# Transposing keys and tokens on TensorE instead of by DMA, and grouping the output and state products, in a gated linear attention plus mixture-of-experts kernel

## The chip, the cores and the metric

One core of a Trainium2 chip. The metric is the device time of one execution in microseconds (us); the time of a kernel is the median of several runs. The engines of the core run side by side, each through its own instructions in order: TensorE (PE, with weight loads as PEld), VectorE (DVE), ScalarE (ACT), GpSimd (POOL) and SyncE (SP), which only issues DMAs here.

## What is computed

For 4 sequences of 2048 tokens of width 256, float32 (8192 tokens): a layer norm, then a gated linear attention and a mixture of 64 experts on the same normalised tokens, and both are added to `x`.

```python
xn = layernorm(x)
q, k, v = xn @ Wq, (xn @ Wk) * DK ** -0.5, xn @ Wv        # 8 heads, DK 128, DV 64
alpha = sigmoid((xn @ Wg + bg) / 16)                      # a decay per head and token
def step(state, inp):                                     # scan over the tokens of a sequence
    state = at[..., None, None] * state + kt[..., None] * vt[:, :, None, :]
    out_t = einsum('bhk,bhkv->bhv', qt, state)
attn = (out * sigmoid(xn @ Wog)) @ Wo
# experts: top 4 of 8 groups, top 8 of 64 experts, at most 256 tokens an expert
y = (silu(xe @ w_gate[e]) * (xe @ w_up[e])) @ w_down[e]   # added back with its weight
return x + attn + moe
```

## The kernel before

The scan over tokens is done in chunks of 128 tokens. A block `s` (32 of them, `block(s)`) is 256 tokens, so two chunks `ck`; the 8 heads go in two halves of 4. One (block, half, chunk) is a unit. For every unit:

- `unit_a`: a matmul `lp` makes the logarithms of the decays between the tokens of the chunk, ScalarE's Relu and Exp make the mask factor `dc` of them (VectorE or GpSimd clears its upper triangle), and 12 matmuls make `sp`, keys times queries.
- `unit_m`: VectorE multiplies `sp` into `dc`.
- `unit_d`: the output products `od<-dc,v` and `od<-qt,state` (float32, 64 columns of the array each) and the state products `od<-vwh,kt` and `od<-vwl,kt` (f16, 128 columns), which need the keys with tokens and features exchanged, `kt`. All go into one PSUM bank `od`. VectorE takes the output out of it with the gate (`oT`), and adds the state part to the decayed state.

Around them, for the next half or block: `queries` and `keys` (each projection `pj` is 12 matmuls; ScalarE takes the high half `qh` or `k`, VectorE the low half `ql` or `k` and, for queries, `qt`, which is scaled by a table `el` that a DMA spreads over the partitions), `values`, `gate` (the `wog` projection), `split_o` (splits `oT` in two for the last product) and `output` (the product with `Wo`). Values are kept as a high and a low part, so `product` issues three matmuls: high by high, high by low, low by high.

`keys` ends with one DMA transpose on SP's queue for both chunks of a half:

```python
kt = ktp.tile([P, NCK * 2 * 4, P], F16, name="kt")
made["kt"] = nc.sync.dma_start(out=kt, in_=k.rearrange("p c a h t -> p (c a h t)"), transpose=True).ins
```

`front(b)` does the layer norm of a batch of 512 tokens (16 batches) and transposes the tokens in the same way, from `x16` into `xT`, on SP's queue; `xT` goes to DRAM and comes back block by block as `xs`. `lg` are the routing logits on `xT`.

`block` writes the order of these parts down by hand. Between them stand 12 calls of `step()` per block. In the first part of the run each `step` drives the side work of the batches: `front`, `decays` and `back` (routing), every one with its due step in the list `side`. When `side` is empty, at the start of a block, the experts begin: PSUM is shared out anew (`share_banks`: four buffers `pj` and two `mo` before, three and three after), and each step advances the experts by a stage: fetch by an indirect DMA on POOL's queue, `expert_in` (which turns the fetched tokens, `xet`, on TensorE), `expert_mid` (`gu`), `expert_out` (`yp`), `expert_add` (a scattering, adding DMA). `finish` adds a block's attention to the output. A scheduler of the framework then sets the final order on each engine out of this order and its own estimate of times; `tc.issue_after(x)` keeps what is issued in it behind the instruction `x`.

PSUM has eight banks: `sp` and `od` have one each, and six are shared between `pj` and `mo`.

Of the kernel before, what the change touches and what calls it, by code (L numbers as in the profile page):

```python
# [8 lines left out]
F32 = mybir.dt.float32  # L9
# [10 lines left out]
P = 128  # L20
NT = 8192
NTL = NT // 128
D = 256
# [48 lines left out]
def gla_moe_kernel(ctx: ExitStack, tc: tile.TileContext, x, Wq, Wk, Wv, Wo, Wg, bg, Wog,  # L72
# [250 lines left out]

    def front(b):
# [54 lines left out]
        n = 2 if b == 0 else RT  # L379
        for t in range(0, RT, n):  # L380
            made["xT"] = nc.sync.dma_start(
                out=xT[:, t:t + n].rearrange("p t a c i -> p (t a c) i"),
                in_=flat[:, t:t + n].rearrange("p t k -> p (t k)"), transpose=True).ins
        nc.sync.dma_start(out=xw_d[rows, 0:D].rearrange("(t p) d -> p t d", p=P),
                          in_=flat.bitcast(F32))
        yield True
        stored = nc.sync.dma_start(out=xT_d[b], in_=xT)
# [5 lines left out]
        for _ in range(6 if b > 2 else 1):  # L393
            yield True
# [220 lines left out]
    def expert_weights(e, m):  # L615
        w = moe["w4"].tile([P, 6, I], F32, name="w", bufs=3)
        nc.sync.dma_start(out=w[:, 0:2], in_=w_gate[e].rearrange("(c p) i -> p c i", p=P))
        nc.sync.dma_start(out=w[:, 2:4], in_=w_up[e].rearrange("(c p) i -> p c i", p=P))
        nc.sync.dma_start(out=w[:, 4:6].rearrange("p c i -> p (c i)"), in_=w_down[e])
        m["w"] = w  # L620
# [234 lines left out]
    def keys(s, half, i):  # L855
# [7 lines left out]
        if i == 1:  # L863
            kt = ktp.tile([P, NCK * 2 * 4, P], F16, name="kt")
            made["kt"] = nc.sync.dma_start(out=kt, in_=k.rearrange("p c a h t -> p (c a h t)"), transpose=True).ins
            B["kt"][half] = kt

    def unit_a(s, half, ck):

        B = blk[s]  # L870
        qh, ql, _ = B["q"][half]
        k = B["k"][half]
# [11 lines left out]
        else:  # L884
            nc.gpsimd.affine_select(out=dc, in_=dc, pattern=[[0, 4], [1, P]], compare_op=ALU.is_ge,  # L885
                                    fill=0.0, base=0, channel_multiplier=-1)
        if (s, half, ck) == (NS - 1, 1, 1):
# [5 lines left out]
        B["dc", half, ck], B["sp"] = dc, sp  # L893
# [8 lines left out]
    def unit_d(s, half, ck):  # L902

        B = blk[s]
        ch = s * NCK + ck
        first = ch % (SEQ // P) == 0
        last = (ch + 1) % (SEQ // P) == 0
        h0 = half * 4
        v, dc, qt = B["v"][ck], B["dc", half, ck], B["q"][half][2]
        od = ps_at.tile([P, 2, 2 * P], F32, name="od", bufs=1)  # L910
        op = od[:, 0].rearrange("p (j i) -> p j i", j=2)
        dp = od[:, 1].rearrange("p (h v) -> p h v", h=4)
        for j in range(2):
            for i in range(2):
                nc.tensor.matmul(op[i * DV:(i + 1) * DV, j, :], lhsT=v[:, h0 + 2 * j + i, :],  # L915
                                 rhs=dc[:, 2 * j + i, :], start=True, stop=first)
            if not first:
                for i in range(2):
                    nc.tensor.matmul(op[i * DV:(i + 1) * DV, j, :], lhsT=state[half][:, 2 * j + i, :],  # L919
                                     rhs=qt[:, ck, 2 * j + i, :], start=False, stop=True)  # L920
        if not last:
            kt, vw = B["kt"][half][:, ck * 8:ck * 8 + 8], B["vw"][ck]
            for i in range(4):
                product(dp[:, i, :], (kt[:, i, :], kt[:, 4 + i, :]),
                        tuple(t[:, h0 + i, :] for t in vw))
        if half == 0:
            B["oT"][ck] = vp_.tile([P, 4, P], F32, name="oT")
        nc.vector.scalar_tensor_tensor(  # L928
            B["oT"][ck][:, half * 2:half * 2 + 2, :], in0=B["og"][:, ck, half * 2:half * 2 + 2, :],
            scalar=1.0, in1=op, op0=ALU.add, op1=ALU.mult)  # L930
        if last:
            return
        new = w2.tile([P, 4, DV], F32, tag=f"state{half}", name=f"state{half}")
        if first:
            nc.vector.tensor_copy(new, dp)
        else:
            B["aux"].tensor_tensor(new, state[half], bc(B["wall"][half][:, ck, :], 2, DV), ALU.mult)
            nc.vector.tensor_tensor(new, new, dp, ALU.add)
        state[half] = new
# [20 lines left out]
    def finish(s):  # L960
# [14 lines left out]
        else:  # L975
            mo = xsp.tile([P, NCK, D], F32, tag="xs", name="mo")
            dst = of[rows, :].rearrange("(t p) d -> p t d", p=P)
            with tc.issue_after(made["kt"]):
# [5 lines left out]

    def block(s):


        n = s + 1 < NS
        if n:
            load_block(s + 1)  # L990
            load_el(s + 1, 0)
        unit_a(s, 0, 0)
        if n:
            queries(s, 1, 0)
        else:
            keys(s, 1, 0)
        unit_m(s, 0, 0)
        step()
        if n:
            keys(s, 1, 0)  # L1000
        else:
            keys(s, 1, 1)
        step()
        unit_d(s, 0, 0)
        if s:
            output(s - 1, 0)
# [4 lines left out]

        unit_a(s, 0, 1)
        queries(s, 1, 1 if n else 0)
        unit_m(s, 0, 1)
        step()
        if n:
            keys(s, 1, 1)
        else:
            queries(s, 1, 1)
        if n:  # L1020
            load_el(s + 1, 1)
            gate(s + 1, 0)
        step()
        unit_d(s, 0, 1)
        step()

        if not n:
            unit_a(s, 1, 0)
            unit_m(s, 1, 0)
# [182 lines left out]
```

## Time and profile before

| | |
|---|---|
| median of 3 runs | 1223.55 us (1221.69 to 1233.08) |
| profiled execution | 1225.81 us, its span 1224.0 us |
| granted TensorE clock, mean | 0.983 |
| TensorE busy | 1148.5 us (94%) |
| VectorE busy | 945.9 us (77%) |
| ScalarE busy | 745.2 us (61%) |
| GpSimd busy | 710.5 us (58%) |
| DMA | 207.15 MB, 315003 packets, 198817 of them under 512 B |

A busy TensorE is a union of pipelined matmuls, so that the time that one costs is the step from its start to the next one's, not its length. An idle time is put down to the event that ended it. In a line of a group stand source line, engine, operation, output and inputs, shape and count, then busy time in us, mean length of one in ns, and the idle time of the engine just before the group with what ended it.

### The profile page before, as it was taken

The numbers are of one execution on the slowest core, as the hardware profiler recorded it, in microseconds if no ns is written. First come the engines' busy times: TensorE is split into PE (matmuls) and PEld (weight loads), VectorE is DVE, ScalarE is ACT, GpSimd is POOL, SyncE is SP. The second block draws the span as 40 slices with busy tenths as digits, with TensorE's granted clock in tenths as the row PEclk, the third lists the DMA queues.
The fourth block names the chain that finished last, engine by engine and source line by source line (L and its number), as shares of the span: only waits on it lengthen the run. The fifth ranks groups of instructions, "written<-read, shape, count | busy, mean of one in ns | idle before, by whom it ended". The sixth has DMA issues, their size and how long they took to land.

```text
span 1224.0 us, 32353 instructions
## 1 busy us (share of the span) xinstructions
PE 1148.5 (94%) x12492; PEld 972.6 (79%) x12503; DVE 945.9 (77%) x2632; ACT 745.2 (61%) x1394; POOL 710.5 (58%) x888
## 2 busy tenths in 40 slices
PE   6889899999899999999979999999999899999998
PEld 6678677777677777787768888888888788888787
DVE  6977676787578666867868898888889778878775
ACT  5567666665566666545445666666676556655664
POOL 1376777765676677553316565466674646565642
PEclk9999999999999999999989999999999899999899
DMA  8579787777677877646667888888898988888855
GB/s 266 143 173 237 184 181 181 181 171 177 146 166 150 182 174 163 154 101 149 148 98 164 177 188 186 196 191 186 177 204 170 184 162 179 171 167 164 204 77 95
DMA packets 315003, 207.15 MB, mean 169 GB/s; under 512 B 198817, under 2 KB 285729, under 8 KB 314145
## 3 DMA queue, kind: packets, MB, share of 16 engines
q1 hardware_dynamic: 281328, 155.52, 53.6%
q0 software_dynamic: 29712, 45.89, 22.2%
q10 hardware_dynamic: 3808, 3.67, 0.9%
q8 instruction: 98, 1.61, 0.6%
q14 instruction: 57, 0.46, 0.1%
HBM read 115.98 MB, written 58.38 MB: 142 GB/s over the span
## 4 chain that ended last, share of the span: by engine, by line
PE 54%; DMA 14%; DVE 12%; POOL 7%; issue 6%; ACT 6%; SPq 1%; POOLq 0%; DVEq 0%; ACTq 0%
PE pj L269 9%; PE pj L271 9%; PE pj L270 9%; DMA kt<-k 8%; DMA el<-el_d 4%; PE od L915 3%; PE od L919 2%; PE gu L269 2%; PE gu L270 2%; PE gu L271 2%; PE xet L630 2%; DVE qt L846 2%; PE sp L269 1%; DVE k L221 1%; PE yp L269 1%
## 5 line engine op out<-in xcount | busy, mean ns | idle before, releaser
L688 POOL DMA_INDIRECT out_dram<-y,idx x128 | 210.4, 1644 | 136.4 <-DMA out_dram<-y,idx 66.6
L610 POOL DMA_INDIRECT xe<-xw_d,idx x128 | 137.0, 1070 | 120.8 <-ACT y L674 41.3
L221 DVE SCALAR_TENSOR_TENSOR ql<-pj,qh 128x512 f16<-128x512 f32 x128 | 87.1, 681 | 64.7 <-ACT qh L220 64.7
L269 PE MATMUL pj<-xs,wq_h 128*128 128x256 f16 x496 | 135.9, 274 | 0.8 <-DVE k L221 0.8
L269 PE MATMUL pj<-xs,wk_h 128*128 128x256 f16 x496 | 136.3, 275 | 0.1
L271 PE MATMUL pj<-xs,wk_l 128*128 128x256 f16 x496 | 136.1, 274 | 0.0
L270 PE MATMUL pj<-xs,wk_h 128*128 128x256 f16 x496 | 136.1, 274 | 0.0
L270 PE MATMUL pj<-xs,wq_h 128*128 128x256 f16 x496 | 135.7, 273 | 0.0
L271 PE MATMUL pj<-xs,wq_l 128*128 128x256 f16 x496 | 135.7, 273 | 0.0
L898 DVE TENSOR_TENSOR dc<-sp,dc 128x512 f32<-128x512 f32 x128 | 87.5, 684 | 43.7 <-POOL dc L885 34.0
L915 PE MATMUL od<-dc,v 128*64 128x128 f32 x1024 | 108.1, 287 | 4.2 <-DVE dc L898 3.1
L220 ACT ACTIVATE qh<-pj 128x512 f16<-128x512 f32 x128 | 76.4, 597 | 45.3 <-PE pj L271 44.8
L220 ACT ACTIVATE k<-pj 128x512 f16<-128x512 f32 x128 | 76.3, 596 | 42.3 <-PE pj L271 41.8
L269 PE MATMUL sp<-qh,k 128*128 128x128 f16 x512 | 97.4, 223 | 3.3 <-ACT k L220 2.4
L919 PE MATMUL od<-qt,state 128*64 128x128 f32 x960 | 99.3, 276 | 0.0
L270 PE MATMUL sp<-ql,k 128*128 128x128 f16 x512 | 96.9, 223 | 1.7 <-DVE ql L221 1.7
L271 PE MATMUL sp<-qh,k 128*128 128x128 f16 x512 | 97.0, 223 | 0.5 <-DVE k L221 0.4
L221 DVE SCALAR_TENSOR_TENSOR k<-pj,k 128x512 f16<-128x512 f32 x128 | 86.8, 678 | 7.9 <-ACT k L220 7.8
L928 DVE SCALAR_TENSOR_TENSOR oT<-og,od 128x256 f32<-128x256 f32 x128 | 52.9, 414 | 47.8 <-PE od L271 46.9
L879 ACT ACTIVATE dc<-lp 128x512 f32<-128x512 f32 x128 | 76.4, 597 | 21.3 <-PE lp L875 19.1
L674 ACT ACTIVATE y<-yp,xe 128x256 f32<-128x256 f32 x128 | 53.7, 471 | 58.4 <-PE yp L271 55.5
L846 DVE SCALAR_TENSOR_TENSOR qt<-pj,el 128x512 f32<-128x512 f32 x128 | 86.7, 678 | 0.0
(401 smaller groups left out, 4244.4 us busy)
## 6 DMA issues: line engine op xcount, KB each, us to landing
el<-el_d SPq DMA_DIRECT2D x64, 512.0 KB
xw_d<-x SPq DMA_DIRECT2D x16, 512.0 KB
xT_d<-xT SPq DMA_DIRECT2D x16, 512.0 KB
out_dram<-in_L_attn_x_dram SPq DMA_DIRECT2D x16, 512.0 KB
w<-in_L_ffn_w_gate_dram SPq DMA_DIRECT2D x64, 128.0 KB
w<-in_L_ffn_w_up_dram SPq DMA_DIRECT2D x64, 128.0 KB
w<-in_L_ffn_w_down_dram SPq DMA_DIRECT2D x64, 128.0 KB
xs<-xT_d SPq DMA_DIRECT2D x31, 256.0 KB
```

What stands on the lines that cost most here:

```text
L220: return (nc.scalar.activation(hi, t, AF.Copy, scale=scale).ins, nc.vector.scalar_tensor_tensor(lo, in0=t, scalar=scale, in1=hi, op0=ALU.m ...
L221: nc.vector.scalar_tensor_tensor(lo, in0=t, scalar=scale, in1=hi, op0=ALU.mult, op1=ALU.subtract).ins)
L269: nc.tensor.matmul(out_, lhsT=a[0], rhs=b[0], start=first, stop=False)
L270: nc.tensor.matmul(out_, lhsT=a[0], rhs=b[1], start=False, stop=False)
L271: return nc.tensor.matmul(out_, lhsT=a[1], rhs=b[0], start=False, stop=last).ins
L610: in_turn(lambda: nc.gpsimd.indirect_dma_start(out=xe[:, f, :], out_offset=None, in_=xw_d[:, :], in_offset=bass.IndirectOffsetOnAxis(ap=id ...
L688: two = [in_turn(lambda: nc.gpsimd.indirect_dma_start(out=of, out_offset=bass.IndirectOffsetOnAxis(ap=idx[:, e, f:f + 1], axis=0), in_=m[" ...
L846: read = nc.vector.scalar_tensor_tensor(qt, in0=pj, scalar=QFIT, in1=two_heads(el, i), op0=ALU.mult, op1=ALU.mult)
L879: nc.scalar.activation(dc, lp, AF.Relu, scale=-1.0)
L898: anchor.append(nc.vector.tensor_tensor(dc, B["sp"], dc, ALU.mult).ins)
L915: nc.tensor.matmul(op[i * DV:(i + 1) * DV, j, :], lhsT=v[:, h0 + 2 * j + i, :], rhs=dc[:, 2 * j + i, :], start=True, stop=first)
L919: nc.tensor.matmul(op[i * DV:(i + 1) * DV, j, :], lhsT=state[half][:, 2 * j + i, :], rhs=qt[:, ck, 2 * j + i, :], start=False, stop=True)
```

## The change

1. Keys: `keys` no longer issues a DMA. A new part `turn_keys(s, half, ck)` transposes the 8 key tiles of a unit on TensorE into a `pj` buffer `kp`; ScalarE copies it to `kt` (before the experts begin, ScalarE and VectorE copy a half each).
2. Tokens: `turn_tokens` transposes the 16 tiles of a batch on TensorE into two `mo` buffers `tp`, and VectorE copies each to `xT`.
3. `unit_d` is split. `outputs(units)` does the output products of two units as one run, held together by `issue_after`, in an `od` bank of their own; `states(units)` does the state products of the two afterwards, in a `pj` buffer `dp`.
4. `unit_l`, the mask factor, is taken out of `unit_a` and stands a step ahead.
5. `block` has a new order: keys first in a half block, then queries, the turned keys, values and gate; `split_o` and `output` move. The first unit stands ahead of the loop over blocks, with a `step()` of its own.

```diff
+    def turn_tokens(x16, xT):
+        for t in range(0, RT, 2):
+            tp = ps["mo"].tile([P, 2, 2, 2, P], F16, tag="mo", name="tp")
...
+                        nc.tensor.transpose(tp[:, t2, a, c, :], x16[:, t + t2, a, c * P:(c + 1) * P], identh)
+            nc.vector.tensor_copy(xT[:, t:t + 2], tp)
...
-        n = 2 if b == 0 else RT
-        for t in range(0, RT, n):
-            made["xT"] = nc.sync.dma_start(
-                out=xT[:, t:t + n].rearrange("p t a c i -> p (t a c) i"),
-                in_=flat[:, t:t + n].rearrange("p t k -> p (t k)"), transpose=True).ins
...
+        if b < 2:
+            turn_tokens(x16, xT)
...
+        if b >= 2:
+            turn_tokens(x16, xT)
+            yield True
...
-        if i == 1:
-            kt = ktp.tile([P, NCK * 2 * 4, P], F16, name="kt")
-            made["kt"] = nc.sync.dma_start(out=kt, in_=k.rearrange("p c a h t -> p (c a h t)"), transpose=True).ins
-            B["kt"][half] = kt
...
+    def turn_keys(s, half, ck):
...
+        kp = ps["pj"].tile([P, 2 * 4, P], F16, tag="pj", name="kp")
+        for i in range(2 * 4):
+            nc.tensor.transpose(kp[:, i, :], k[:, i, :], identh)
...
+        if "at" in moe:
+            nc.scalar.copy(kt, kp)
+        else:
+            nc.scalar.copy(kt[:, 0:4], kp[:, 0:4])
+            nc.vector.tensor_copy(kt[:, 4:8], kp[:, 4:8])
...
+    def outputs(units):
+
+        od = ps_at.tile([P, 2, 2, P], F32, name="od", bufs=1)
+
+        begun = ExitStack()
+        for n, (s, half, ck) in reversed(list(enumerate(units))):
...
+                    mm = nc.tensor.matmul(od[i * DV:(i + 1) * DV, n, j, :], lhsT=v[:, h0 + 2 * j + i, :],
+                                          rhs=dc[:, 2 * j + i, :], start=True, stop=first)
+                    if i == j == 0:
+                        begun.enter_context(tc.issue_after(mm.ins))
...
+    def states(units):
...
+        dp = ps["pj"].tile([P, 2, 4, DV], F32, tag="pj", name="dp")
+        for n, (s, half, ck) in enumerate(units):
+            kt, vw = blk[s]["kt"][half][:, ck * 8:ck * 8 + 8], blk[s]["vw"][ck]
+            with tc.issue_after(made["od"]):
+                for i in range(4):
+                    product(dp[:, n, i, :], (kt[:, i, :], kt[:, 4 + i, :]),
+                            tuple(t[:, half * 4 + i, :] for t in vw))
```

The new order of the first half block, in `block`:

```diff
+        states(done)
+        if s:
+            split_o(s - 1, 1)
...
+        unit_l(s, 0, 1)
+        keys(s, 1, 0)
+        step()
+        unit_a(s, 0, 1)
+        keys(s, 1, 1)
+        unit_l(s, 1, 0)
+        step()
+        unit_m(s, 0, 1)
+        queries(s, 1, 0)
+        step()
+        queries(s, 1, 1)
+        turn_keys(s, 1, 0)
+        if s:
+            output(s - 1, 1)
+        step()
...
+        if n:
+            values(s + 1, 0)
+        unit_a(s, 1, 0)
+        turn_keys(s, 1, 1)
+        if s:
+            gate(s, 1)
+        step()
+        unit_m(s, 1, 0)
+        done[:] = (s, 0, 1), (s, 1, 0)
+        outputs(done)
+        step()
```

The second half block has the same order for the other half of the heads, with the next block's projections.

## The prediction

> **What bounds the kernel now.** I read the page first: engine totals, then the chain of work that ended last, then the windows of 30 us, the groups by line, the waits, and last TensorE's timeline at the edges of the `od` products.
>
> ```profile
> PE 1148.5 (94%) x12492; PEld 972.6 (79%) x12503; DVE 945.9 (77%) x2632; ACT 745.2 (61%) x1394; POOL 710.5 (58%) x888
> ...
> PE 54%; DMA 14%; DVE 12%; POOL 7%; issue 6%; ACT 6%; SPq 1%; POOLq 0%; DVEq 0%; ACTq 0%
> ```
>
> TensorE is busy for 1148.5 of 1224.0 us and holds most of the chain. Only 75.5 us of it are idle, so added TensorE work is paid in full unless it takes the place of a wait. The windows (columns: span, busy time and instructions of PE, PEld, DVE, ACT, POOL, granted clock, DMA share, GB/s) show two halves:
>
> ```profile
> 450.00:480.00 30.00, 29.13 (x341) 23.57 (x339) 20.61 (x69) 19.93 (x35) 22.44 (x39) 1.00 0.68 163
> ...
> 600.00:630.00 30.00, 22.57 (x252) 19.19 (x252) 19.13 (x60) 10.51 (x19) 10.21 (x10) 0.89 0.71 114
> ...
> 660.00:690.00 30.00, 30.00 (x346) 26.48 (x343) 27.39 (x71) 18.45 (x37) 19.17 (x14) 1.00 0.87 183
> ...
> 960.00:990.00 30.00, 27.86 (x275) 24.83 (x273) 21.62 (x56) 15.10 (x32) 17.92 (x14) 0.91 0.79 151
> ```
>
> In the second half, with the experts, TensorE is full (30.00 of 30) except in a few holes, after which the granted clock falls as well (0.89, 0.91). In the first half it loses a little in every window. The groups name the waits (busy, mean ns, idle before, releaser):
>
> ```profile
> L269 PE MATMUL od<-vwh,kt 128*128 128x64 f16 x480 | 58.6, 197 | 23.1 <-DMA kt<-k 23.0
> L269 PE MATMUL pj<-xs,wog_h 128*128 128x256 f16 x248 | 67.9, 274 | 8.5 <-DVE qt L846 7.3 <-ACT res L958 1.2
> L271 PE MATMUL pj<-wo_h,ol 128*128 128x256 f32 x256 | 73.9, 289 | 6.7 <-POOL ol L946 6.5
> L269 PE MATMUL lg<-gwz,xT 128*128 128x72 f16 x128 | 14.1, 198 | 3.4 <-DMA xT<-x 3.4
> ```
>
> The holes are the state products waiting for the transposed keys: 23.0 us. The chain in order of time shows how late such a transfer lands, beside an `el` broadcast, which also fills 512 KB:
>
> ```profile
> 186.60 5.99 DMA el<-el_d
> ...
> 607.79 15.61 DMA kt<-k
> ```
>
> **What the change adds on TensorE.** 32 blocks x 2 halves x 2 chunks x 8 key tiles are 1024 transposes, and 16 batches x 16 token tiles are 256: 1280, each with its own weight load; the built order has exactly these more. The experts' inputs are turned in the same way (f16, 128x128):
>
> ```profile
> 1006.31 0.28 PE L271 MATMUL yp<-wh,hl 128*128 128x256 f32 x1
> 1006.43 0.62 PE L630 MATMUL xet<-identh,xe 128*128 128x128 f16 x8
> 1006.98 0.44 PE L919 MATMUL od<-qt,state 128*64 128x128 f32 x4
> 1007.25 0.39 PE L915 MATMUL od<-dc,v 128*64 128x128 f32 x4
> 1007.47 0.39 PE L919 MATMUL od<-qt,state 128*64 128x128 f32 x4
> 1007.79 0.20 PE L269 MATMUL od<-vwh,kt 128*128 128x64 f16 x1
> ```
>
> One takes 220 ns, but they are pipelined: 8 take 0.62 us, so the step is (0.62 - 0.22) / 7 = 0.057; I use 0.056, the step of `sp`, which has the same shape (three in 0.17 in the same timeline). 1280 x 0.056 = +71.7 us. TensorE executes in order, so all of it lies on the path where TensorE is full.
>
> The Trainium skill, "TensorE: Matmul & The Clock Gate", Part 4, puts such a transpose at about 275 ns in a kernel and says that it does not count as work for the clock gate. Taken as a spacing, 1280 x 0.275 would be 352 us; the row above gives 0.056, and the window from 660 to 690, which holds `xet` runs, has a granted clock of 1.00, so the row decides.
>
> **Output products as one group.** `od<-dc,v` and `od<-qt,state` use 64 columns (128*64), all around them 128. Inside, a group of four records steps by 0.22 (1007.25 to 1007.47); at the exit it is 0.32 (1007.47 to 1007.79), +0.10; at the entry 0.21 between a projection (1005.27, step 0.11) and the first `od` (1005.48), +0.10. A visit costs 0.20 us. In the built order of before there are 148 visits, mostly of 8 instructions and some broken up; in that of after 67, 54 of them of 16. 81 x 0.20 = -16 us. Bounds: nothing, where a visit is entered after a wait anyway, and -16.
>
> **Waits that go.** Keys: -23.0, since `kt` now comes out of a ScalarE copy that stands, in the order, ahead of the `od` group that precedes its use (bounds: -23.0, and 0 if another wait takes its place, which is R3). Tokens: -3.4. Clock: the windows after the key holes grant 0.89, 0.97, 0.91, 0.94, 0.99, 0.90; 30 x (0.11 + 0.03 + 0.09 + 0.06 + 0.01 + 0.10) = 12.0 us of clock, of which I take -9, as part of it fell on an idle TensorE (bounds -12 and 0). `output` of both chunks now stands about 9 us of TensorE work behind its `split_o`, where before the second one stood beside it: -6.5. The `wog` projection waits for a PSUM buffer that `qt` frees, and `qt` waits for `el`; on SP's queue that load now has no key transpose ahead of it (64 x 3.67 us of issue, median of the group by tile): -5 of 7.3 (bounds 0 and -7.3).
>
> The Trainium skill, "Advanced Engine Details and Errata", X-Bar Transpose (TRN2), speaks against the change: transposing DMAs are as fast as regular ones. The chain has 15.6 us for a key transfer where the equal-sized `el` took 6.0. By the rule the keys would land early enough without TensorE, the waits would have another cause, and the sum would be 1224 + 72 - 16 = 1280; I go by the rows.
>
> **Copies out of PSUM.** They are new work on the two engines beside:
>
> ```profile
> L638 DVE CAST xel<-xet 128x512 fp32r<-128x512 f16 x64 | 43.7, 683 | 1.0 <-ACT xeh L637 0.8
> L637 ACT CAST xeh<-xet 128x512 fp32r<-128x512 f16 x64 | 38.0, 593 | 10.2 <-PE xet L630 8.3 <-PE od L271 1.0 <-issue 0.3
> L377 ACT CAST x<-xt 128x1024 f16<-128x1024 f32 x14 | 14.5, 1033 | 0.0
> ```
>
> By the built order: ScalarE 66 x 0.59 + 62 x 1.03 = 103 us (745 to 848, under 70%). VectorE 66 x 0.68 = 45 and 32 token copies of 128x1024, not in the trace: between 0.68 (one of half the size) and 1.37 (two); I take 1.25, 40 us. All 85 us fall in the first half, where VectorE was busy 437 of the first 600 us (73%); it goes to about 87%. Cover: in the window 660 to 690 VectorE was at 27.39 of 30 and TensorE lost nothing, so 0 is the lower end. Queued behind such a copy are the low halves `ql`, `k` and `qt`, which free the projection's PSUM buffers, and the `dc` product that the next `od` group waits for. The upper end: TensorE's idle of the first 600 us, 49.5, less 7 for keys and tokens and 10 for the first window, is 32; a doubling costs +32. I take +5, nearer the row at 91%.
>
> PSUM: `kp` (4) and `dp` (2) join 18 other tiles per block in the `pj` pool, with 4 buffers, then 3. Waits for these buffers were only the 8.5 us of `wog`, so I price this at 0, with R3 as its other end. On SP the 81 transposes go, nothing is added; POOL's queue keeps its order, though the experts begin one block earlier (66 half copies of keys: 2 + 16 x 4).
>
> **Sum**, against the profiled execution's span: 1224.0 + 71.7 - 16 - 23.0 - 3.4 - 9 - 6.5 - 5 + 5 = 1237.8. That execution took 1225.81, 1.8 more than its span; the median, 1223.55, lies 2.3 below it. So 1237.8 + 1.8 - 2.3 = 1237 us, 1.1% slower. About 1% is also what a measurement of this kernel can tell from no change.
>
> **Rivals.**
> R1, VectorE becomes the pace of the first half. For: 87% there, in lockstep with a full TensorE through 4 PSUM buffers; the first half already waits on `ql`, `k`, `qt`. Against: 91% in the second half at no loss. Price +32 in place of +5: 1264.
> R2, not slower: the longer distances of the new order (mask factors and keys a step ahead, one `od` visit per half block) empty the remaining waits too. TensorE's idle less what I took off is 75.5 - 23 - 3.4 - 6.5 - 5 = 37.6, of which 10 are the start; if 26 go and VectorE adds nothing, 1237 - 26 - 5 = 1206. It decides from about 14 us of them on. For: those waits (`dc`, `ql`, `k`) are all first-half distances of a few matmuls. Against: VectorE's load grows there.
> R3, a wait takes the key wait's place: `kp` holds a `pj` buffer through a 1.03 us copy behind other ScalarE work. At half a copy per turn in the second half 62 x 0.5 = +31 at worst; at a third of that, 1247. Against: ScalarE is at 63% there.
>
> **How the numbers follow.** Forecast 0.40 (its own range 1224 to 1251), R1 0.22, R2 0.24, R3 0.14. Of the forecast 0.01 is faster by over 1%, 0.17 within 1%, 0.22 slower; R1 is all slower; R2 0.19 and 0.05; R3 0.07 within and 0.07 slower. Together 0.20, 0.29, 0.51. The range runs from 1208, R2 nearly whole, to 1264, R1 whole.
>
> **What would show it.** Right: `kp` and `tp` step by 0.056; the `kt` wait is gone from TensorE and the windows after 600 have clock 1.00; DMA share falls; VectorE 85 us more. The second half gets shorter and the first longer. Wrong: over 15 us of TensorE idle behind VectorE in the first half (R1), idle in all under 35 us (R2), or `pj` groups waiting on the ScalarE copy of `kt` (R3).

## The result and the profile after

The changed kernel takes 1285.84 us (median of 4 runs, 1277.83 to 1288.44); the kernel before, run beside it, 1227.99 us. The ratio is 1.0463, with a 95% interval of 1.0386 to 1.0540: slower. The forecast was 1237 us, with a range to 1264. The direction was right; the size was missed by 49 us. Of the kernels below only order_later had timed executions in a slower state with a lower granted clock (two of eight); its ratio leaves them out, its median does not.

The page of the profile after (engine busy time, one DMA queue with packets, MB and share, and the engines of the chain that ended last):

```profile
PE 1203.5 (94%) x13783; PEld 1043.5 (81%) x13783; DVE 997.4 (78%) x2733; ACT 832.4 (65%) x1522; POOL 712.1 (55%) x885
...
q1 hardware_dynamic: 114896, 113.57, 28.5%
...
PE 53%; DVE 18%; POOL 13%; ACT 6%; issue 4%; DMA 4%; SPq 1%; another core or an unknown queue 0%; POOLq 0%; DVEq 0%; ACTq 0%
```

DMA has gone from 14% of the chain to 4%, and this queue from 53.6% of the DMA engines' time to 28.5%. The line of that queue before:

```profile
q1 hardware_dynamic: 281328, 155.52, 53.6%
```

VectorE and GpSimd together now hold 31% of the chain (19% before). TensorE's idle time is 1286.7 - 1203.5 = 83.2 us, against 75.5 before, although the waits for transposed keys are gone. The same windows as before; the work in them is not quite the same, since block 16, for one, begins 48 us later in the change (span, PE, PEld, DVE, ACT, POOL, granted clock, DMA share, GB/s):

```profile
450.00:480.00 30.00, 27.71 (x340) 23.39 (x338) 23.07 (x73) 18.29 (x34) 18.98 (x31) 1.00 0.45 132
600.00:630.00 30.00, 25.50 (x250) 20.31 (x248) 26.45 (x80) 15.80 (x27) 13.96 (x15) 0.94 0.54 157
660.00:690.00 30.00, 28.66 (x309) 25.22 (x308) 23.87 (x60) 20.74 (x40) 14.25 (x11) 1.00 0.56 122
960.00:990.00 30.00, 29.63 (x335) 26.05 (x333) 24.16 (x60) 22.11 (x43) 17.06 (x13) 1.00 0.65 152
```

The hole in the last window is filled (27.86 at a clock of 0.91 before), that at 600 only in part (22.57 at 0.89 before), and windows that were full lose a little (450: 29.13, 660: 30.00 before). The groups show both sides (busy, mean ns, idle before, releaser):

```profile
L940 PE MATMUL od<-dc,v 128*64 128x128 f32 x1024 | 102.2, 282 | 9.6 <-DVE dc L924 9.6
L270 PE MATMUL sp<-ql,k 128*128 128x128 f16 x512 | 96.2, 219 | 16.5 <-DVE ql L221 15.6 <-issue 0.4
L879 PE MATMUL kp<-identh,k 128*128 128x128 f16 x1024 | 84.0, 219 | 11.2 <-DVE k L221 8.7 <-ACT dc L898 2.0 <-issue 0.4
L271 PE MATMUL pj<-wo_h,ol 128*128 128x256 f32 x256 | 72.8, 284 | 0.4 <-DVE ol L985 0.4
L269 PE MATMUL pj<-xs,wog_h 128*128 128x256 f16 x248 | 67.6, 273 | 0.4 <-ACT res L997 0.4
L269 PE MATMUL dp<-vwh,kt 128*128 128x64 f16 x480 | 50.7, 195 | 0.0
L269 PE MATMUL lg<-gwz,xT 128*128 128x72 f16 x128 | 14.7, 199 | 0.0
```

The last four lines are the waits that the forecast took off, and all four are gone. The first three are waits that were small before (below), and the `kp` group is new.

```profile
L915 PE MATMUL od<-dc,v 128*64 128x128 f32 x1024 | 108.1, 287 | 4.2 <-DVE dc L898 3.1 <-DVE state L938 0.9
L270 PE MATMUL sp<-ql,k 128*128 128x128 f16 x512 | 96.9, 223 | 1.7 <-DVE ql L221 1.7
```

**A balance of TensorE's time.** To see where the time went I followed every step from one matmul's start to the next one's. The usual step of a shape is work (0.056 us for 128x128 f16, 0.109 for 128x256 f16, 0.110 for an output product); up to 0.104 more at the edge of the 64-column products is the change of tile; what is left under a granted clock below 0.9 is half clock, except steps longer by 0.3 us or more; the rest is a stall from 0.15 us on, and small below that. I cut the run at VectorE's first `dc<-sp` product of block 0 and of block 16. What I call the first half is blocks 0 to 15, with layer norm and routing beside them; the second runs from there to the end, with the experts. All in us:

| kernel, half | length | work | of it `kp`, `tp` | tile | clock | stalls | small |
|---|---|---|---|---|---|---|---|
| before, first | 515.7 | 451.5 | 0 | 13.3 | 5.0 | 36.4 | 8.7 |
| after, first | 563.3 | 496.3 | 41.1 | 7.7 | 1.6 | 49.4 | 8.3 |
| before, second | 660.9 | 580.2 | 0 | 15.2 | 10.3 | 33.2 | 18.2 |
| after, second | 675.9 | 608.7 | 27.3 | 6.0 | 2.7 | 36.9 | 16.8 |

Both halves got longer: +47.6 and +15.0. In both, the transposes stand as work to nearly their full price, tile changes and clock give back what was forecast, and the stalls are not shorter but longer.

### The profile page after: what moved, and what is told of

The parts are those of the page before. It is cut to its first block, busy times and chain, and to the rows that moved or that the text cites. A ratio compares the mean times of both kernels' runs of the same rounds, so it can differ in the third digit from the quotient of the medians.

```text
span 1286.7 us, 34811 instructions
## 1 busy us (share of the span) xinstructions
PE 1203.5 (94%) x13783; PEld 1043.5 (81%) x13783; DVE 997.4 (78%) x2733; ACT 832.4 (65%) x1522; POOL 712.1 (55%) x885
## 3 DMA queue, kind: packets, MB, share of 16 engines
q1 hardware_dynamic: 114896, 113.57, 28.5%
## 4 chain that ended last, share of the span: by engine, by line
PE 53%; DVE 18%; POOL 13%; ACT 6%; issue 4%; DMA 4%; SPq 1%; another core or an unknown queue 0%; POOLq 0%; DVEq 0%; ACTq 0%
PE pj L269 8%; PE pj L271 8%; PE pj L270 8%; PE od L940 3%; DMA el<-el_d 3%; PE od L946 2%; PE kp L879 2%; PE gu L269 2%; PE gu L271 2%; PE xet L639 2%; PE gu L270 2%; POOL ol L985 2%; POOL state L976 2%; DVE ql L221 2%; DVE k L221 2%
## 5 line engine op out<-in xcount | busy, mean ns | idle before, releaser
L270 PE MATMUL sp<-ql,k 128*128 128x128 f16 x512 | 96.2, 219 | 16.5 <-DVE ql L221 15.6
L940 PE MATMUL od<-dc,v 128*64 128x128 f32 x1024 | 102.2, 282 | 9.6 <-DVE dc L924 9.6
L946 PE MATMUL od<-qt,state 128*64 128x128 f32 x960 | 94.8, 275 | 0.0
L879 PE MATMUL kp<-identh,k 128*128 128x128 f16 x1024 | 84.0, 219 | 11.2 <-DVE k L221 8.7
L834 ACT ACTIVATE v<-pj 128x512 f32<-128x512 f32 x64 | 38.2, 598 | 78.5 <-PE pj L271 69.3
```

The costliest lines, as they stand in the source:

```text
L270: nc.tensor.matmul(out_, lhsT=a[0], rhs=b[1], start=False, stop=False)
L879: nc.tensor.transpose(kp[:, i, :], k[:, i, :], identh)
L940: mm = nc.tensor.matmul(od[i * DV:(i + 1) * DV, n, j, :], lhsT=v[:, h0 + 2 * j + i, :], rhs=dc[:, 2 * j + i, :], start=True, stop=first)
L946: mm = nc.tensor.matmul(od[i * DV:(i + 1) * DV, n, j, :], lhsT=state[half][:, 2 * j + i, :], rhs=qt[:, ck, 2 * j + i, :], start=False, sto ...
```

## The experiments

Every kernel below was timed beside the kernel before; "first" and "second" are the halves as defined above, from one profiled execution of each. How far single executions scatter can be read from kernels whose code is the same in the second half: the change, one_by_one and mask_dve have 672.0 to 678.0 us there, the four kernels named order_ 632.7 to 643.5, the kernel before and tokens_old_order 660.9 and 667.1. Differences under some 10 us between such halves are therefore not told from chance. The profiled executions of tokens_old_order and order_pen_pool lay 9 and 10 us above their medians, that of keys_twice 7 below.

| kernel | median, us | ratio (95%) | first | second |
|---|---|---|---|---|
| before | 1225 to 1230 | 1 | 515.7 | 660.9 |
| the change | 1285.84 | 1.0463 (1.0386 to 1.0540) | 563.3 | 675.9 |
| order_alone | 1260.81 | 1.0231 (1.0186 to 1.0277) | 575.8 | 637.7 |
| turned_old_order | 1294.97 | 1.0507 (1.0458 to 1.0555) | 568.2 | 677.7 |
| keys_old_order | 1294.21 | 1.0561 (1.0500 to 1.0622) | 566.0 | 673.7 |
| tokens_old_order | 1232.44 | 1.0031 (0.9999 to 1.0063) | 524.3 | 667.1 |
| keys_unturned | 1291.05 | 1.0478 (1.0431 to 1.0525) | 596.1 | 647.7 |
| keys_twice | 1360.02 | 1.1051 (1.0997 to 1.1104) | 599.2 | 703.7 |
| copies_short | 1281.96 | 1.0453 (1.0392 to 1.0515) | 561.2 | 668.2 |
| dc_three | 1281.98 | 1.0447 (1.0408 to 1.0486) | 560.6 | 669.2 |
| mask_dve | 1301.03 | 1.0598 (1.0558 to 1.0637) | 579.9 | 672.0 |
| one_by_one | 1279.89 | 1.0428 (1.0389 to 1.0467) | 548.2 | 678.0 |
| order_pen_pool | 1235.07 | 1.0068 (1.0038 to 1.0098) | 550.5 | 643.5 |
| order_pen_single | 1223.69 | 1.0018 (0.9977 to 1.0058) | 541.7 | 632.7 |
| order_later | 1235.85 | 1.0054 (1.0023 to 1.0085) | 542.9 | 641.5 |
| change_later | 1325.33 | 1.0814 (1.0786 to 1.0843) | 584.0 | 689.9 |
| mixed_dma | 1231.55 | 1.0043 (1.0015 to 1.0071) | 515.5 | 665.4 |
| mixed_turned | 1249.51 | 1.0174 (1.0117 to 1.0231) | 516.4 | 685.9 |
| mixed_fixed | 1215.96 | 0.9922 (0.9894 to 0.9950) | 516.3 | 648.2 |

### The parts of the change one at a time

**order_alone**: the new order and the grouped products, with both transposes left to DMA.

```diff
-        turn_keys(s, 1, 0)
...
+        if i == 1:
+            kt = ktp.tile([P, NCK * 2 * 4, P], F16, name="kt")
+            made["kt"] = nc.sync.dma_start(out=kt, in_=k.rearrange("p c a h t -> p (c a h t)"), transpose=True).ins
```

> The new order and the grouping alone; keys and tokens are transposed by DMA as before. Theory O (the new order makes the new TensorE waits: queries stand just ahead of the products that read them): the waits for ql, k and dc come back without any transposes on TensorE, so slower than before by 10 to 40 us, about 1250. Theory T (TensorE pays for the transposes and the order costs nothing): the 16 us of fewer od visits are gained, about 1210. Theory C (the copies out of PSUM crowd ScalarE and VectorE): as T, about 1210.

Second half 23 us shorter, first half 60 us longer. In the second half the key waits are gone although the keys still travel by DMA: the whole run has 0.2 us of them.

```profile
L269 PE MATMUL dp<-vwh,kt 128*128 128x64 f16 x480 | 54.1, 199 | 0.2 <-DMA kt<-k 0.2
```

The new order, in which the keys are projected first in a half block, does this without TensorE; its parts were not tried apart. The balance of the second half is clock -10.3, tile -8.9, stalls only -2.2: 22.1 us of key waits went, and others of nearly the same sum came. The time, 1260.81, is within what theory O allowed, 10 to 40 us slower. In the first half stalls went from 36.4 to 83.9, nearly all at one group, and the half clock from 5.0 to 22.1:

```profile
L928 PE MATMUL od<-dc,v 128*64 128x128 f32 x1024 | 109.6, 301 | 66.7 <-DVE dc L912 66.1 <-issue 0.3
```

**turned_old_order**: the kernel before with both transposes on TensorE (two `turn_keys` per half block, put between the parts of the old order).

```diff
+        turn_keys(s, 0, 0)
         step()
...
+        turn_tokens(x16, xT)
```

> The old order with one unit a group, keys and tokens transposed on TensorE, copies as in the change; turn_keys stands just ahead of the step before each unit_d. Theory O: 72 us of TensorE work less 23 + 3 of DMA waits and about 10 of clock, and no new waits: about 1262. Theory T: the same without grouping, about 1290 or above, as the change is 1286 with the 16 us of grouping gained. Theory C: the copies bring the new waits here too, ql and k waits above 20 us, about 1290.

First half +52.5, of which `kp` and `tp` are 41.6 us of work; second half +16.8 with 27.0 us of them, as the 22.1 us of key waits go. The stalls of both halves fall by only 4.4 us, 69.6 to 65.2. So in the old order too the transposes are paid in full, as theory T had it, and most of what the key waits leave is taken by others: that does not need the new order.

**keys_old_order** and **tokens_old_order**: the same with only the keys, or only the tokens, on TensorE.

```diff
 keys_old_order, against turned_old_order
-            turn_tokens(x16, xT)
+            made["xT"] = nc.sync.dma_start(
 tokens_old_order, against the kernel before
+            turn_tokens(x16, xT)
```

> The kernel before with the keys alone transposed on TensorE, in the old order. Paid in full: first half 516 + 29 - 4 = 541, second 661 + 28 + 10 - 30 (the key waits and the clock after them) = 669, in all about 1260. If the first half hides them: about 1235.

> The kernel before with the tokens alone transposed on TensorE (256 transposes, 14 us, and 32 copies on VectorE, 0.68 us each, all in the first half). Paid in full: first half 516 + 14 - 3 = 527, in all about 1238. Hidden in the first half's waits: about 1225. If VectorE's copies pace it too: up to 1260.

The keys are nearly the whole cost: 1.0561 against 1.0031. The tokens' 13.4 us of work make the first half 8.6 us longer in an execution that took 9 us more than the median; by the ratio of the timed runs they cost some 4 us. The keys make it 50 us longer for 28.2 us of transposes; 25 us were expected (541), and 1260 in all. New waits came with them; the largest (before, this group waited 0.6 us):

```profile
L887 PE MATMUL lp<-mv,aj 128*128 128x512 bf16 x128 | 49.4, 386 | 20.5 <-DVE qt L846 18.8 <-issue 0.8 <-DVE rep L517 0.7
```

`lp` needs a `pj` buffer, and `qt` is what frees one. With `kp` in the same pool a buffer comes round later: on this reading, it is the price that I had put at 0. No run gave `kp` a buffer of its own, so that the pool is the cause is argued and not shown.

### What the keys cost in the second half

**keys_unturned**: the change without the key transposes; the copies read `k` directly from SBUF, so that the state products work on keys that were not turned.

```diff
-        for i in range(2 * 4):
-            nc.tensor.transpose(kp[:, i, :], k[:, i, :], identh)
...
-            nc.scalar.copy(kt, kp)
+            nc.scalar.copy(kt, k)
```

> The change, without the 1024 key transposes and their PSUM buffers: the copies to kt read k itself (the state products use keys that are not turned). The copies and the order stay. Theory T: the whole 57 us go, 1229. Theory O: the waits at ql and dc stay and grow into part of the gap: 25 to 45 us go, about 1250. Theory C: nearly no gain beyond 57 x the share of full TensorE, about 1250, and ql waits stay as they are.

**keys_twice**: each key transpose is issued twice into the same place.

```diff
             nc.tensor.transpose(kp[:, i, :], k[:, i, :], identh)
+            nc.tensor.transpose(kp[:, i, :], k[:, i, :], identh)
```

> The change with every key transpose done twice into the same place: 1024 more, 57 us of TensorE work and nothing else. Theory T: 1286 + 57 = 1343. Theory O: in the second half in full (29), in the first half part of it falls into the waits for ql and dc: 1320 to 1335. Theory C: as T or O, between 1320 and 1343.

None of the three theories fits either run as a whole: keys_unturned was to be at 1229 to 1250 us and took 1291.05, and keys_twice was to be at 1343 at most and took 1360.02, 74 us more than the change for 57 us of work. The second half alone reads more simply. It holds 62 x 8 = 496 key transposes, 27.8 us at the step of 0.056. Taking them away shortens it by 675.9 - 647.7 = 28.2 us, doubling them lengthens it by 703.7 - 675.9 = 27.8. Within the scatter both agree with the full price (keys_unturned also gives up the `kp` buffers, and its copies read SBUF). The step itself stands in the timeline of the change; eight in 0.45 us:

```profile
715.90 0.61 PE L879 MATMUL kp<-identh,k 128*128 128x128 f16 x8
716.35 0.27 PE L269 MATMUL pj<-xs,wog_h 128*128 128x256 f16 x1
```

The first half of keys_unturned is no measure of the transposes, though: it is 33 us longer than the change's, without their work. Its stalls (90.1) and half clock (21.9) are near those of order_alone (83.9 and 22.1), and the next group of runs shows one of their causes.

**copies_short**: the change, with the key copies cut to 4 of 128 columns, into buffers filled once; the state products read what was filled in.

```diff
-            nc.scalar.copy(kt, kp)
+            nc.scalar.copy(kt[:, 0:8, 0:4], kp[:, 0:8, 0:4])
```

> The change with copies of 4 of 128 columns out of each kp tile in place of all (the rest of kt is a constant): TensorE's work and the order stay, about 55 us of ScalarE and 20 us of VectorE copy work go. If the copies pace the first half (theory C): 10 to 25 us less there, and about 10 less in the second: 1255 to 1265. If the order and TensorE's work alone do it: about 1276, 10 less in the second half only.

Nothing in the first half (-2.1), 7.7 us in the second, where ScalarE makes the whole copy of 1.02 us. In the timed runs this can't be told from nothing (1.0453 against 1.0463), and dc_three, which has all its copies, comes out at 669.2 in the second half, as short as copies_short with 668.2. So a price of the copies is not shown.

From the kernel before through order_alone and keys_unturned to the change the second half goes 660.9, 637.7, 647.7, 675.9: -23 with the new order, +10 with the copies, +28 with the transposes. That these add up to the +15 of the change is no check, since each is the difference to the one before it. Against the scatter the first and the last are clear; the 10 is not.

### What the order costs in the first half

Costs do not add up in this half: the new order alone makes it 60 us longer, the transposes in the old order 52, and the change, which has both, 48. Part of the new order's cost alone must therefore be absent from the change.

**one_by_one**: before the experts begin, the first unit's output products stand on their own and not in a group with the second's. **dc_three**: a third buffer for `dc`. **mask_dve**: GpSimd's causal mask of `dc` goes to VectorE in the first half too, as load for VectorE.

```diff
 one_by_one
         queries(s, 1, 1)
+        if "at" not in moe:
+            outputs([(s, 0, 1)])
...
-        outputs(done)
+        outputs(done if "at" in moe else done[1:])
 dc_three
-    dcp = ctx.enter_context(tc.tile_pool(name="dcp", bufs=2))
+    dcp = ctx.enter_context(tc.tile_pool(name="dcp", bufs=3))
 mask_dve
-        if "at" in moe:
+        if True:
             nc.vector.tensor_tensor(dc, dc, bc(u_le, 1, 4), ALU.mult)
```

> The change, but before the experts begin the output products of each unit stand by themselves: those of the first unit of a pair right behind the second query projection, those of the second at the old place. Theory L (all 16 products of a group hang on the latest dc): the first half gets shorter by 10 to 25 us although it has 30 more od visits, 1262 to 1275. Theory G (GpSimd's and VectorE's side work sets the pace of the first half): no gain, 1285 to 1292. Theory D (two dc buffers, both held by a group until it ends): a part of L's gain, about 1275.

> The change with three buffers for dc in place of two, nothing else. Theory D: mask factors are made ahead of the end of the group, 10 to 25 us less, 1262 to 1275. Theories L and G: no change, 1280 to 1290.

> The change with the upper triangle of dc cleared by VectorE in the first half too, as in the second; GpSimd is out of the chain of dc. Theory G: 64 x 0.7 us leave the chain through GpSimd: 10 to 30 us less, 1256 to 1275. Theory L: within 8 us of the change. If VectorE's load sets the pace: 64 x 0.68 = 43 us more work on it, 10 to 40 us slower.

Apart from each other the output products take 15 us off the first half (stalls 49.4 to 23.4, tile changes 7.7 to 14.1). In the timed runs 6 us are left of it, with intervals that overlap (1.0428 against 1.0463). What went is mainly the wait for `ql`: 15.6 us in the change, 3.8 here. The wait for `dc`, on which theory L had put the gain, stayed as it was, 9.6 and 9.9:

```profile
L270 PE MATMUL sp<-ql,k 128*128 128x128 f16 x512 | 96.0, 220 | 4.4 <-DVE ql L221 3.8 <-issue 0.2
L940 PE MATMUL od<-dc,v 128*64 128x128 f32 x1024 | 103.3, 283 | 9.9 <-DVE dc L924 9.9
```

The edit puts the first unit's output products behind the second query projection, and so ahead of the scores that read that projection's `ql`: the distance from the queries to the scores got longer. A third buffer takes off 3 us: `dc` isn't short of buffers. The mask, 62 x 0.68 = 42 us more for VectorE, adds 16.6 us, although GpSimd is rid of it. So VectorE's load does weigh in the first half, by 0.4 us per us in this run; at that rate the change's 48 us of copies would be 19 us. Taken out directly, most of the key copies show far less: copies_short has 17 us less of them on VectorE and 27 us less on ScalarE in this half, for 2.1 us.

**order_pen_pool**: order_alone with one routing instruction moved from VectorE to GpSimd.

```diff
-        nc.vector.tensor_scalar(pen, gm, BIG, -BIG, ALU.mult, ALU.add)
+        nc.gpsimd.tensor_scalar(pen, gm, BIG, -BIG, ALU.mult, ALU.add)
```

> The order alone (DMA transposes) with the routing's pen computed on GpSimd in place of VectorE. If pen's 2.9 us, nine times, each held up the dc product behind it because VectorE waits until GpSimd is idle: 15 to 25 us less than the order alone, about 1240. If od waits for dc for another reason: about 1260.

It came out of the timeline of order_alone. VectorE, GpSimd and TensorE in turn, the same stretch (start, us, instruction, idle before):

```profile
391.07 0.98 DVE L512 TENSOR_SCALAR gm<-rank 128x32 f32<-128x32 f32 x1
392.09 2.86 DVE L514 TENSOR_SCALAR pen<-gm 128x32 f32<-128x32 f32 x1
394.87 0.68 DVE L912 TENSOR_TENSOR dc<-sp,dc 128x512 f32<-128x512 f32 x1
```

```profile
389.89 2.13 POOL L387 TENSOR_TENSOR x<-xt,x 128x1024 f16<-128x1024 f32 x1
391.97 1.25 POOL L991 DMA_DIRECT2D out_dram<-res  x1
392.81 1.51 POOL L840 TENSOR_TENSOR vw<-v,w_end 128x512 f32<-128x512 f32 x1
393.83 1.07 POOL L516 TENSOR_TENSOR tmp<-sfc,gm 128x256 f32<-128x256 f32 x1
```

```profile
395.60 0.44 PE L928 MATMUL od<-dc,v 128*64 128x128 f32 x4 [4.26 <-DVE dc L912]
```

`pen` touches 32 numbers per partition and takes mostly 0.18 us elsewhere; here it ends only when GpSimd's row of instructions ends, and the `dc` product that the output products wait for stands behind it in VectorE's queue. The 16 of them sum to 23.4 us in order_alone, 24.4 in keys_unturned, 4.8 before and 4.1 in the change. With `pen` on GpSimd the first half is 25 us shorter. The change itself escapes this. It is not the copies that make the difference, since keys_unturned has them and does not escape. In the change GpSimd has the same three instructions beside `pen`, but `tmp` ahead of `vw`, and eight times `pen` takes 0.23 us there, as here (VectorE, then GpSimd):

```profile
206.20 0.23 DVE L514 TENSOR_SCALAR pen<-gm 128x32 f32<-128x32 f32 x1
```

```profile
205.58 1.26 POOL L1003 DMA_DIRECT2D out_dram<-res  x1
206.43 1.09 POOL L516 TENSOR_TENSOR tmp<-sfc,gm 128x256 f32<-128x256 f32 x1
207.02 1.51 POOL L840 TENSOR_TENSOR vw<-v,w_end 128x512 f32<-128x512 f32 x1
```

Why GpSimd's order comes out differently was not settled.

**order_pen_single**: the edits of order_pen_pool and one_by_one together, still with DMA transposes.

> The order alone (DMA transposes), pen on GpSimd, and before the experts begin the output products of each unit by themselves. If the rest of the order's cost in the first half is the group behind the latest dc: the first half falls from 550 to 520 to 535 us, in all about 1215. If it is the distance from the queries to their products, or something else: within 8 us of 550, in all about 1235.

Another 9 us off, between the two expectations; the whole is level with the kernel before. Its second half is the shortest of all here (632.7), but its first half is still 26 us longer than before, and output products still wait 34.9 us for `dc`. Two runs asked whether that place is the cause.

**order_later** and **change_later**: on top of order_pen_single and of one_by_one, the second unit's output products and the state products stand behind the next key projection, before the experts begin.

```diff
-        outputs(done if "at" in moe else done[1:])
+        if "at" in moe:
+            outputs(done)
+        else:
+            late.append(done[1])
...
         keys(s + 1, 0, 0)
+        if late:
+            outputs([late.pop()])
+            states(done)
+            split_o(s, 0)
         step()
```

> As order_pen_single (new order, transposes by DMA, pen on GpSimd, output products ungrouped before the experts), but before the experts the second unit's output products and the state products stand a key projection later, so that more of TensorE's work lies between a unit's scores and its output products. order_pen_single took 1223.7 us, its first half 541.7 us, and its output products still wait 34.9 us for dc there. Theory K (the place of the output products right behind the latest dc is what the new order still costs): the wait goes nearly whole, first half 508 to 520 us, the whole 1192 to 1202 us (0.975 to 0.983). Theory L (the queues beside TensorE set the pace of the first half, and the wait for dc is only where that shows): the wait reappears at other instructions (sp, lp, the projections), first half 535 to 542, the whole 1217 to 1225 us (0.995 to 1.002).

> The same edit in the change itself, on top of one_by_one (the change with output products ungrouped before the experts: 1279.9 us, first half 548.2 us, its output products wait 7.0 us for dc there). Theory K: only these 7 us are left to win, first half 540 to 543, the whole 1272 to 1276 us. Theory L: nothing, first half 546 to 550, the whole 1278 to 1283 us.

The wait for `dc` went, and nothing was won. TensorE's waits between 60 and 600 us (what waits, for what, sum, times, longest), first in order_pen_single, then in order_later:

```profile
PE od L928 <- DVE dc L912: 34.9, 29, 3.2
PE dp L269 <- DMA kt<-k: 5.5, 3, 4.4
```

```profile
PE pj L269 <- DVE k L221: 16.2, 9, 3.5
PE dp L269 <- DMA kt<-k: 7.9, 5, 3.6
PE pj L269 <- ACT dc L886: 6.3, 4, 2.0
PE od L928 <- DVE dc L912: 4.0, 4, 1.5
```

The stalls of the first half are 46.2 and 46.5 us: the wait moved to the projections, which wait for a buffer that the split of the keys frees. Theory K, that the place of the output products is the cost, falls. Theory L, that the engines beside TensorE set the pace and the wait shows wherever TensorE asks too early, fits better: the first half, 542.9, is at the edge of its 535 to 542, the ratio, 1.0054, a little above its range. Which engine sets the pace was not shown. In change_later the same edit even costs 36 us (stalls 23.4 to 58.4), which neither theory expected; which queue it upsets stays open, and with that theory L itself. So do the 26 us that are left of the order's cost in the first half: 9.8 of stalls, 9.3 of half clock, 6.5 of slower steps.

### The order only where it pays

**mixed_dma**: the old order for blocks 0 to 16, the new order and the groups from block 17 on, where the experts begin; transposes by DMA. **mixed_turned**: the same, with the keys turned on TensorE from there on. **mixed_fixed**: mixed_dma, with `finish`'s load behind the newest key transpose, as in the kernel before.

```diff
+        if s < FROM:
+            block_old(s)
+            continue
 mixed_fixed, against mixed_dma
-            with tc.issue_after(made["el"]), tc.issue_after(made["w"]):
+            with tc.issue_after(made["kt"]), tc.issue_after(made["w"]):
```

> No transposes on TensorE. Blocks 0 to 16 in the old order with one unit a group, blocks 17 to 31 (with the experts) in the new order with two units a group. Reading by stages: the first half as before (563 us to block 16), the second as in the run of the order alone (638 us from block 16 in place of 661): about 1203, faster than before by 1.5 to 2%. If the stages do not add up (the second half of the order alone was short because its first half was long): about 1225.

> Old order and DMA transposes up to block 16; from block 17 on the new order with the keys transposed on TensorE. If transposes are paid in full where TensorE is full, and the copies cost ScalarE 10 us there: 60 x 8 x 0.056 = 27 + 10 more than the same with DMA transposes (1215): about 1252. If they are hidden in waits: about 1220.

> As the run of old order first, new order second, DMA transposes; in finish the load of the last block's output is now issued behind the last key transposes, which it kept waiting on SP's queue (16.1 us of TensorE's idle time in the last block). If the stages add up: 1231 - 16 = 1215, about 1% faster than before. If the last block waits for something else then: 1225 to 1231.

mixed_dma won in the middle (blocks 17 to 29 take 540 us, against 562 before) and lost it near the end, in one wait of 16.1 us. TensorE's group, and the wait on SP's queue that stands ahead of that key transpose (L1046 is the load of `finish`, which waits for the experts' adds):

```profile
L270 PE MATMUL dp<-vwh,kt 128*128 128x64 f16 x224 | 23.9, 196 | 16.1 <-DMA kt<-k 16.1
```

```profile
SPq L1046 <- DMA out_dram<-y,idx: 27.0, 2, 19.6
```

With the load behind the transpose, mixed_fixed takes 1215.96 us, 0.9922 of the kernel before (0.9894 to 0.9950), and beats both kernels. mixed_turned, which puts only the keys on TensorE in the same place, is 33.6 us slower than that; its 480 transposes at 0.056 us are 26.9 of it. So the timed runs, too, show them paid in full.

## Why the prediction was wrong in size

By the steps of its sum, over both halves:

- **Transposes, +71.7.** Right: 41.1 + 27.3 = 68.4 us of work between the cuts (32 of the 1280 lie ahead of the first), and the second half shows the price twice more, by taking them away and by doubling them. The Trainium skill, "TensorE: Matmul & The Clock Gate", Part 4, has some 275 ns for one transpose as its length; in this trace the length is 219 ns, and what counts here is the step, 0.056 us. That transposes are no work for the clock gate no run here can show: the mean granted clock of the change is 0.994, but its transposes stand among other products.
- **Visits, -16.** Right: 28.5 to 13.7, -14.8.
- **Clock, -9.** Right: 15.3 to 4.3, -11.0.
- **Waits, -23.0 - 3.4 - 6.5 - 5 + 5 = -32.9.** This is the step that failed. The four waits went, as said. But the stalls of both halves went from 69.6 to 86.3 us, +16.7. Against -32.9 that is 49.6 us, all of the miss; work beyond the transposes (+4.9) and small steps (-1.8) add little.

The term that was mis-sized is "+5" for new waits. With 37.9 us of waits taken off and the stalls 16.7 us higher, the new waits come to 54.6. I had reckoned them by VectorE's load alone, and had read the window at 660 us, where VectorE was at 91% and TensorE lost nothing, as cover. It says that a busy VectorE is no harm while its products are due late; it says nothing of an order in which they are due at once. In the new order the queries stand right ahead of the scores that use them, and the output products behind the newest `dc`. I counted the longer distances (keys, mask factors) as gains and did not go through the ones that became shorter. The stalls of the first half by what ended them, before and after: `ql` under 0.8 and 15.3 us, `k` 2.4 and 10.9, `dc` 2.1 and 6.9; against that `ol` 7.9 and under 0.7, `qt` 7.3 and 0.9, tokens 3.6 and none. For `ql` two pairs of runs support this: the wait goes when the first unit's output products are put between the queries and the scores (the change to one_by_one, and order_pen_pool to order_pen_single, 7.3 to 3.3 us). For `k` and `dc` it is argued. The order is also not the whole of it: in turned_old_order 27.5 us of waits for keys and tokens went as well, and the stalls fell by 4.4.

The half by half forecast, "the second half gets shorter and the first longer", failed in its first part. The second half's 22.1 us of key waits went, and waits for which the profile names no releaser grew from 5.5 to 20.1 us, in many pieces. Order_alone already has 11.2 of them and 8.6 behind ScalarE's `dc`, so part of this may be the order's. What makes them late was not settled: for the second half the cause of the new waits stays open.

**PSUM at 0.** Probably too low: in the old order `lp` waited 18.8 us for `qt`, as I read it for a `pj` buffer. In the change those do not appear; there the projections, the `kp` and the `sp` groups wait.

**Copies.** ScalarE's 103 us came as priced. VectorE's were 48 us and not 85:

```profile
L887 DVE COPY kt<-kp 128x512 f16<-128x512 f16 x66 | 27.1, 411 | 11.7 <-ACT kt L886 11.6
L331 DVE COPY xT<-tp 128x1024 f16<-128x1024 f16 x32 | 20.9, 682 | 3.6 <-PE tp L330 3.6
```

```profile
L884 ACT COPY kt<-kp 128x1024 f16<-128x1024 f16 x62 | 63.1, 1018 | 9.7 <-PE kp L879 6.0 <-PE yp L271 0.9 <-remote 0.9
L886 ACT COPY kt<-kp 128x512 f16<-128x512 f16 x66 | 38.3, 582 | 6.8 <-PE kp L879 5.2
```

I had priced them by a cast that writes 32-bit numbers; a copy from f16 to f16 of the same size takes 0.41 and not 0.68.

**The rivals.** R1 came nearest. Its sign, over 15 us of TensorE idle behind VectorE in the first half, was there, and about its size: the stalls that VectorE's instructions ended rose from 18 to 42 us in that half (R1 had 27 more than the forecast). Its cause was that only in part, if at all. VectorE did not fill up: between 60 and 560 us it was busy for 370.4 us (74%), against 362.4 before, where I had expected 87%; and with most of the key copying taken out the first half stays at 561.2. order_alone, without a single copy more, has the longer stalls behind VectorE. R3, waits on the ScalarE copy, is not shown: the `pj` groups of the change wait 0.6 us for it, and the 7.7 and 10 us that the second halves differ by are within the scatter. The second half did find other waits in the place of the key wait, but not this one. R2 fell: no idle went beyond the waits named.

The rule in the Trainium skill, "Advanced Engine Details and Errata", X-Bar Transpose (TRN2), that transposing DMAs are as fast as regular ones, led to a sum of 1280, close to 1285.84, with the reason that another wait would stay. That it came so close is luck. Other waits did stay, but the key waits were real, and order_alone shows their cure: the same DMA transposes, asked for earlier, leave 0.2 us of 23. Nor do the two lines of q1 agree with the rule. With the transposes 155.52 - 113.57 = 41.95 MB left the queue and, by its shares (53.6% of 1224.0 us, 28.5% of 1286.7), 656 - 367 = 289 us of the 16 engines' time. That is an estimate of 145 GB/s for them, where the rest of the queue moves 310.

## What to carry to other kernels

When a full engine waits for a DMA, first try to start the transfer earlier: here, beside the experts, the new order did away with the waits for the keys without TensorE, and TensorE's transposes cost their full 28 us in that half, where TensorE is full. A new order is judged stage by stage, by the distances that it shortens as well as by those that it lengthens; the same order won 23 us beside the experts and lost 60 beside the routing. A removed wait should not be counted as won until one has gone through what is due next behind it: take a sum of waits in one stage as the thing to forecast, not the one line that is the largest.

## What the runs showed of the hardware

A short VectorE instruction from SBUF to SBUF can be held until a whole row of GpSimd instructions has ended: in order_alone `pen` took 2.38 to 2.87 us eight times, in place of 0.18, and each time it ended within 0.1 us of the end of the same GpSimd product, `tmp<-sfc,gm`, as in the stretch shown. The Trainium skill, "SBUF — State Buffer", section "SBUF: two separate sides", says that VectorE in some modes and GpSimd share a pair of ports, and that whoever comes first holds it for its whole instruction while the other blocks. The trace fits that VectorE blocks. It goes further in length: the hold covered several GpSimd instructions in a row and not one. A row without a pause is not enough for it: in the change eight of the `pen` instructions stand beside the same three GpSimd instructions in another order and take 0.23 us. Which instructions of GpSimd hold it was not tried apart.

Nearly halving the load of DMA queue q1 brought no gain that shows. In turned_old_order it takes 28.2% of the engines' time in place of 53.6%, and the stalls of both halves are 65.2 us against 69.6, although 27.5 us of key and token waits were among those 69.6. The transposes and copies came in the same run, so what the lighter queue is worth by itself is not told.
